# A scan kernel on one core: order of a PSUM seed, two gate tiles kept in SBUF, earlier stores, and group statistics on GpSimd

## The chip, the cores and the metric

The kernel runs on one core of one Trainium2 chip. The metric is device time in microseconds (us) of one execution, the median of several. One more execution was recorded by the profiler; every duration of a single instruction comes from that one.

## What is computed

The input x is 4 x 128 x 96 x 96, float32. It is normalized in 32 groups of channels, then four sequences of each image (rows, rows backwards, columns, columns backwards) go through one block, and the four results are mixed and added to x:

```python
t = _grouped1x1(x, in_proj_w, in_proj_b, G)
u, gate = (t[:, :HID], t[:, HID:])
u = jax.nn.silu(u)
u = lax.conv_general_dilated(u, dw_w, ..., feature_group_count=HID)   # 5 taps
s = _conv1x1(u, ssm_in_w)
a = DMIN + (DMAX - DMIN) * jax.nn.sigmoid(_conv1x1(u, ssm_delta_w, ssm_delta_b))
bb = jnp.tanh(_conv1x1(u, ssm_b_w, ssm_b_b)); cc = jnp.tanh(_conv1x1(u, ssm_c_w, ssm_c_b))
# hst: h[i] = a[i] * h[i-1] + bb[i] * s[i]
u = u + _conv1x1(cc * hst + ssm_d[None, :, None] * s, ssm_out_w)
u = _grouped1x1(u * jax.nn.sigmoid(gate), mix_w, mix_b, G)
return _conv1x1(u, out_proj_w, out_proj_b)
```

## The kernel before

The engines are TensorE (PE), VectorE (DVE), ScalarE (ACT), GpSimd (POOL) and SyncE (SP), whose queue issues nearly all DMAs. The order of every engine's work is written out by hand.

**Pairs, steps, phases.** The work is cut into 192 pairs t = 0 to 191. A pair is the same quarter (residue p of the column index) of a block of lines in two opposite directions, s = 0 and 1. Four pairs (k = 0 to 3, residues 1, 2, 3, 0) make a step, six steps a phase of 24 pairs, and eight phases cover four images, columns (V) before rows (H). Below m = t mod 24. Back-end work (ssm_out, gating, final products) lags by six pairs: in pair t it is that of pair n = t - 6. Front-end work (in_proj and silu) runs four pairs ahead. Pairs 0 to 7 are emitted by `pair`, the others by `pair_on`.

**Fresh and copied steps.** In the first three steps of a phase silu is computed. As the opposite direction sees the same lines in mirrored order, the last three steps reuse it: it is stored to DRAM (`keep_silu`, L473) and loaded again (`load_silu`). The gates, tanh of a projection of x, go the same way: computed in the first half of a phase, stored to `kept`, and in the second half pair n loads that of pair `mirror(n)` (12 takes 9, 13 takes 8, 14 takes 11, 15 takes 10). There are two gate tiles in SBUF, `gates[n % 2]` (`tile_of`, L597). The gates of the first three pairs of the next phase are computed early, in m = 17, 18 and 19, into the tile `shared` and stored from there. A tap that reaches into the neighbouring 32 channels' rows needs copies of silu's edge rows: `keep_lone` (L699) stores them with four DMAs and `load_lone` (L706) loads them into the tile `lone`, which `add_lone` (L710) reads in pairs of k = 2 and 3. `keep_lone` is issued in the pair of k = 0 of a fresh step, and its load in k = 1.

**One pair in `pair_on` (L1044), in PE's order.** If a front is due, in_proj into banks 7, 6, 2, 3; `conv` with the matrix `band`; two `accumulate` calls, the final products of the pair before (`w_fin`), whose results ACT copies to `ys` and POOL adds to `acc`; `conv_less` with the matrix `less`, if the pair is not single (k = 0 and 1), followed by ACT's copy of the sum to u; a block of eight matmuls, four gates and four ssm_out; `proj`, the four projections of u. A pair with a front is called fronted here (m = 20 to 23 and 0 to 7), one that is neither fronted nor single **long** (m = 8, 9, 12, 13, 16, 17), one that is single and not fronted short. ssm_out adds onto a seed: `under` (L557) has ACT copy u into ssm_out's banks (0 and 1 for s = 0, 2 and 3 for s = 1). Banks 0 and 1 are also where DVE sums the taps 1 to 4 (L765), ahead of the seed, after ACT's first tap (L763). `gating` (L649) on DVE multiplies ssm_out with the gate. On ACT a long pair runs: the projections' tanh and copies (L802, L805, L810), the scaling of s (`scale_s`, L820), the seed of s = 1, a ys copy, u's copy (L738), the seed of s = 0 (L560), a ys copy, two tanh of gates (L564), the first tap, two more gates (L570).

**Statistics.** During the V phase of an image, DVE takes bn_stats of the next image's chunks (L412). Then `stats_finish` (L181) is a generator: in each pair of k = 2 and 3 of the following H phase `pair_on` runs two of its pieces between the final products and conv_less, on PE, DVE and POOL (three Newton steps for the inverse root), so that the scaled weights `wn` and biases `bnorm` are there four pairs ahead of the next image.

**SP's order at the end of a pair.** The store of the new gate (L1143, which waits for its last tanh), the x_in loads for later gates (`load_gate`), the chunk of x for the statistics (`load_chunks`), and the gate of pair n + 2 (`load_kept`); after a pair of k = 2 this load goes to the start of the next.

Of the kernel before, what the change touches and what calls it, by code (L numbers as in the profile page):

```python
# [47 lines left out]
P = 128  # L48
# [20 lines left out]
def conv_preact_kernel(  # L69
# [111 lines left out]
    def stats_finish(b):  # L181

        if b != b0:
            yield
# [7 lines left out]
        if b != b0:  # L197
            yield
# [14 lines left out]
        if b != b0:  # L213
            yield
        inv = sp.tile([P, 2], F32, tag="inv", name=f"inv_{b}")
        if b == b0:
            std = sp.tile([P, 2], F32, tag="err", name="std")
            nc.scalar.activation(std, var, AF.Sqrt)

            nc.scalar.activation(first_table, std[:, 0:1], AF.Silu)  # L220
            nc.vector.reciprocal(inv, std)
        else:
            bits = inv.bitcast(I32)
            nc.vector.tensor_single_scalar(bits, var.bitcast(I32), 1, ALU.logical_shift_right)
            nc.vector.tensor_scalar(bits, bits, -1.0, float(0x5F3759DF), ALU.mult, ALU.add)
            err = sp.tile([P, 2], F32, tag="err", name=f"err_{b}")
            for turn in range(3):
                if turn:
                    yield
                    yield  # L230
                nc.gpsimd.tensor_mul(err, inv, inv)
                nc.gpsimd.tensor_mul(err, err, var)
                nc.gpsimd.tensor_scalar(err, err, -0.5, 1.5, ALU.mult, ALU.add)
                nc.gpsimd.tensor_mul(inv, inv, err)
        yield
        if b != b0:
            yield
# [4 lines left out]

# [3 lines left out]


        pb = bank(free[0])
        product(pb[:, 0:4], wn, gm4)
        if b == b0:  # L250
            for g in range(4):
                for q in range(R):
                    mm(pb[:, 4 + g : 5 + g], q, wn[0:32, 32 * g : 32 * g + 32], mean[0:32, :], True, True)
            nc.vector.tensor_sub(bn, b_in, pb[:, 0:8])
        else:
            nc.vector.tensor_sub(bn[:, 0:4], b_in[:, 0:4], pb[:, 0:4])
            spread = sp.tile([P, 4], F32, tag="spread", name=f"spread_{b}")
            shift = sp.tile([P, 1], F32, tag="shift", name=f"shift_{b}")
            nc.vector.tensor_copy(shift, pb[:, 0:1])  # L259
            yield  # L260
            nc.vector.tensor_scalar_mul(spread, gmask, shift)
            yield
            pq = bank(free[0])
            for q in range(R):
                mm(pq[:, 0:4], q, id32, spread, True, True)
            nc.vector.tensor_sub(bn[:, 4:8], b_in[:, 4:8], pq[:, 0:4])
            yield
        nc.vector.tensor_scalar_mul(bn[:, 2:4], bn[:, 2:4], 0.5)


# [307 lines left out]
    def sigmoids(bi, to):  # L578
        bn = stats[units[bi]["b"]][1]
        n = bi // 2  # L580
        gv = gates[n % 2]
# [15 lines left out]
    def tile_of(n):  # L597
        return gates[n % 2]

    def load_kept(n):  # L600
# [3 lines left out]
        if n < NU // 2 - R and m is not None:  # L604
            nc.sync.dma_start(tile_of(n), kept[n // NP % 2][m])
# [120 lines left out]
    def conv_less(i, banks):  # L726
        step, p = units[i]["step"], units[i]["p"]
        sil, k, b0 = blocks(step), less_of(p), min(banks)
        for g in range(4):
            for s in range(2):  # L730
                r = less_rows(s, p)
                mm(bank(b0 + s), g, less[r, p, g, :], columns(step, sil[s][r, g, :], k),
                   False, True)
        if banks == PROJ:
# [164 lines left out]
    later, soon = [], []  # L899
# [14 lines left out]
    def pair(t):  # L914
# [49 lines left out]
        ending = old and t % (2 * NP) > NP + NP // 2  # L964

        def stats_piece(at_end=False):
            if later and k > 1 and at_end == ending and t % (2 * NP) not in (27, 39):
                next(later[0], None)

        if not ahead:  # L970
            free[0] = w[1]
            stats_piece()
# [18 lines left out]
        if ahead:  # L991
            accumulate(waiting.pop(0), w[1], *final)()
            free[0] = w[0]
            stats_piece()
# [13 lines left out]
        if un["order"] == "V" and un["b"] + 1 < B and un["st"] == NS - 1 and k == R - 1:  # L1008
            later[:] = [stats_finish(un["b"] + 1)]
# [20 lines left out]
        if ending:  # L1030
            free[0] = FRONT[0]
            stats_piece(True)
# [11 lines left out]
    def pair_on(t):  # L1044
# [38 lines left out]
        stats_chunks(t)  # L1083
# [30 lines left out]
        if later and k > 1:  # L1114
            free[0] = w[0]
            for _ in range(2):
                next(later[0], None)
        if fronted:
            if not single:
                conv_less(i, banks)  # L1120
            scale_s(i - 2)
# [12 lines left out]
        gate_of(0, 1, 5)  # L1134
        for s in range(2):
            gating(bi, s)
            if s == 0 and gated is not None:
                tanh_one(gated, to, 1, 1, 4)
                tanh_one(gated, to, 0, 1, 5)
        first_tap(i + 2)  # L1140
        if gated is not None:
            tanh_both(gated, to, 0, 6)
            nc.sync.dma_start(kept[gated // NP % 2][gated % NP], to)  # L1143
# [5 lines left out]
        if un["order"] == "V" and un["b"] + 1 < B and un["st"] == NS - 1 and k == R - 1:  # L1149
# [300 lines left out]
```

## Time and profile before

| | us |
|---|---|
| median of 3 runs (1782.19 to 1784.2) | 1783.57 |
| the profiled execution | 1788.7 |
| its span, first to last instruction | 1787.0 |

The granted TensorE clock was 0.997 over the span. 417.89 MB went through the DMA engines. A row of a group or of the timeline names line, engine, operation and `out<-in` tiles. `psum<-u,w_fin` on PE is `accumulate`, `psum<-sil,band` conv, `psum<-sil,less` conv_less, `psum<-x_in,wn` a gate (32*128) or in_proj (32*32), `psum<-t,main` ssm_out, `psum<-u,main` proj. Line 135 is a helper that emits most matmuls, so tiles tell them apart. Each matmul of the program shows as two instructions.

### The profile page before, as it was taken

The numbers are of one execution on the slowest core, as the hardware profiler recorded it, in microseconds if no ns is written. First come the engines' busy times: TensorE is split into PE (matmuls) and PEld (weight loads), VectorE is DVE, ScalarE is ACT, GpSimd is POOL, SyncE is SP. The second block draws the span as 40 slices with busy tenths as digits, with TensorE's granted clock in tenths as the row PEclk, the third lists the DMA queues.
The fourth block names the chain that finished last, engine by engine and source line by source line (L and its number), as shares of the span: only waits on it lengthen the run. The fifth ranks groups of instructions, "written<-read, shape, count | busy, mean of one in ns | idle before, by whom it ended". The sixth has DMA issues, their size and how long they took to land.

```text
span 1787.0 us, 54377 instructions
## 1 busy us (share of the span) xinstructions
PE 1739.9 (97%) x22618; PEld 661.0 (37%) x22618; DVE 1496.9 (84%) x1526; ACT 1492.7 (84%) x2551; POOL 1423.3 (80%) x1477
## 2 busy tenths in 40 slices
PE   6999999999999999999999999999999999999998
PEld 3334333443334433344333443334433343334433
DVE  6888888887889888888778988888877888888887
ACT  4888888888888888888888888888888888888875
POOL 3578788877878878887777888888787888888886
PEclk9999999999999999999999999999999999999999
DMA  7775975558996688456798688744889749756464
GB/s 238 213 248 193 304 232 166 202 189 278 292 335 233 233 261 243 143 198 230 249 329 301 217 276 262 225 160 163 276 257 316 260 151 311 239 183 198 166 208 176
DMA packets 193814, 417.89 MB, mean 234 GB/s; under 512 B 17312, under 2 KB 154912, under 8 KB 193568
## 3 DMA queue, kind: packets, MB, share of 16 engines
q1 hardware_dynamic: 193424, 414.37, 70.5%
q8 instruction: 179, 2.93, 0.7%
q14 instruction: 67, 0.55, 0.1%
q10 hardware_dynamic: 144, 0.04, 0.0%
HBM read 250.58 MB, written 163.76 MB: 232 GB/s over the span
## 4 chain that ended last, share of the span: by engine, by line
PE 81%; DMA 8%; ACT 4%; DVE 3%; POOL 2%; issue 1%; SPq 1%; DVEq 0%; ACTq 0%; POOLq 0%
PE psum L135 68%; PE psum L548 8%; PE psum L528 5%; DMA kept<-shared 2%; DVE psum L765 1%; DMA x_in<-in_xs 1%; DMA out<-acc 1%; DMA lone<-edge 1%; ACT sil L498 1%; DMA edge<-sil 1%; ACT psum L560 1%; DVE u L664 1%; DMA xs<-in_xr 1%; ACT psum L763 1%; ACT shared L564 0%
## 5 line engine op out<-in xcount | busy, mean ns | idle before, releaser
L765 DVE SCALAR_TENSOR_TENSOR psum<-sil,small,psum 128x768 f32<-128x768 f32 x576 | 589.0, 1023 | 51.7 <-ACT psum L763 26.3
L135 PE MATMUL psum<-u,main 128*32 128x384 f32 x6144 | 538.2, 491 | 13.8 <-ACT shared L564 7.2
L135 PE MATMUL psum<-u,w_fin 128*32 128x384 f32 (+1 forms) x6192 | 543.1, 485 | 1.6 <-ACT ys L872 0.4
L664 DVE SCALAR_TENSOR_TENSOR u<-gate,psum 128x768 f32<-128x768 f32 x376 | 341.8, 950 | 181.2 <-PE psum L548 65.8
L891 POOL TENSOR_TENSOR acc<-ys,acc 128x384 f32<-128x384 f32 x375 | 411.2, 1119 | 21.2 <-ACT ys L874 4.5
L845 POOL TENSOR_TENSOR t<-t,t 64x384 f32<-64x384 f32 (+1 forms) x192 | 235.3, 1225 | 137.8 <-DVE t L839 84.3
L135 PEld LDWEIGHTS psum<-u,w_fin 128*32 128x32 f32 x6192 | 194.5, 110 | 313.0 <-issue 233.9
L135 PEld LDWEIGHTS psum<-u,main 128*32 128x32 f32 x6144 | 181.4, 110 | 342.6 <-issue 219.6
L560 ACT COPY psum<-u 128x768 f32<-128x768 f32 x380 | 298.2, 799 | 9.2 <-DVE u L664 4.4
L135 PE MATMUL psum<-sil,band 128*32 128x384 f32 x3072 | 285.5, 488 | 0.3 <-ACT gate L570 0.3
L846 POOL TENSOR_TENSOR t<-t,t 64x384 f32<-64x384 f32 (+1 forms) x192 | 272.3, 1418 | 15.1
L812 POOL TENSOR_SCALAR t<-tm 64x384 f32<-64x384 f32 x191 | 177.1, 927 | 110.3 <-ACT tm L802 84.0
L763 ACT ACTIVATE psum<-sil,small 128x768 f32<-128x768 f32 x191 | 172.5, 903 | 86.0 <-DVE u L664 83.6
L548 PE MATMUL psum<-t,main 32*128 32x384 f32 x1536 | 209.6, 524 | 4.5 <-ACT psum L560 3.3
L813 POOL TENSOR_TENSOR t<-t,tm 64x384 f32<-64x384 f32 x192 | 196.7, 1025 | 16.8 <-ACT t L805 1.6
L765 DVE SCALAR_TENSOR_TENSOR u<-sil,small,psum 128x768 f32<-128x768 f32 x192 | 194.9, 1015 | 6.9
L498 ACT ACTIVATE sil<-psum,bnorm 128x385 f32<-128x385 f32 x384 | 192.2, 584 | 3.9 <-PE psum L135 1.8
L528 PE MATMUL psum<-x_in,wn 32*128 32x384 f32 x768 | 167.9, 495 | 3.6 <-DVE shift L259 1.4
L135 PEld LDWEIGHTS psum<-sil,band 128*32 128x32 f32 x3072 | 89.8, 108 | 171.3 <-issue 60.6
L874 ACT COPY ys<-psum 128x384 f32<-128x384 f32 x281 | 129.5, 477 | 14.9 <-PE psum L135 11.8
L564 ACT ACTIVATE gate<-psum,bnorm 128x384 f32<-128x384 f32 x148 | 85.8, 581 | 57.1 <-PE psum L528 56.8
L802 ACT ACTIVATE tm<-psum,small 128x384 f32<-128x384 f32 x192 | 111.1, 579 | 11.6 <-PE psum L135 3.4
(105 smaller groups left out, 1512.0 us busy)
## 6 DMA issues: line engine op xcount, KB each, us to landing
sil<-sil SPq DMA_DIRECT2D x128, 770.0 KB, 6.5
gate<-kept SPq DMA_DIRECT2D x113, 768.0 KB, 6.2
kept<-gate SPq DMA_DIRECT2D x75, 768.0 KB, 3.6
lone<-edge SPq DMA_DIRECT2D x46, 770.0 KB, 7.3
x_in<-in_xs SPq DMA_DIRECT2D x194, 96.2 KB, 3.9
edge<-sil SPq DMA_DIRECT2D x96, 192.5 KB, 6.9
out<-acc SPq DMA_DIRECT2D x48, 384.0 KB, 7.9
kept<-shared SPq DMA_DIRECT2D x21, 768.0 KB, 5.2
```

The source lines that it names most:

```text
L135: nc.tensor.matmul(o[r, : rhs.shape[-1]], lhsT, rhs, start=start, stop=stop, skip_group_check=True)
L498: nc.scalar.activation(sils[step][:, s, j, g, :], bank(bk)[:, : N + 1], AF.Silu, bias=bn[:, 1:2] if j else bn[:, 4 + g : 5 + g],)
L528: nc.tensor.matmul(bank(to)[:, :N], stats[un["b"]][0][r, s, :], x_in[s][r, q, off : off + N], start=True, stop=True)
L548: nc.tensor.matmul(bank(ssm(bi, s) + j)[:, :N], w_so[r, bass.ts(j, P)], z[r, :], start=bi not in seeded, stop=True, skip_group_check=True)
L560: nc.scalar.copy(psum[:, ssm(bi, s) : ssm(bi, s) + 2, :N], us[bi][:, s])
L664: nc.vector.scalar_tensor_tensor(v, g, 1.0, pz, ALU.add, ALU.mult)
L763: nc.scalar.activation(part, src, AF.Copy, scale=w_tap[:, 0:1])
L765: nc.vector.scalar_tensor_tensor(us[i][:, :, 1, :] if k == K - 1 else part, src, w_tap[:, k : k + 1], part, ALU.mult, ALU.add,)
L813: nc.gpsimd.tensor_mul(ta[0:64, p, :], tb[0:64, :], tm[0:64, :])
L845: engine.tensor_mul(ta[0:64, p, r], tb[64:P, r], ta[64:P, p, r])
L846: engine.tensor_add(tb[0:64, r], ta[0:64, p, r], tb[0:64, r])
L891: adder.tensor_add(part, y, part)
```

## The change

1. In long pairs the seed of s = 0 is issued on ACT ahead of u's copy; `conv_less` can leave the copy out and `copy_u` does it later.
2. `tile_of` shifts by one at the middle of each phase, and the gates of pairs 10 and 11 of a phase (`stays`) are neither stored nor loaded. As written, pairs 11 and 12 then share one tile: the load for pair 12, at the end of pair 10, goes into the tile in which pair 11's gate was written, and pair 11's gating comes behind it in the program. Pair 13's load goes into pair 10's tile, and pairs 14 and 15 read the two tiles as these loads left them. So pairs 11, 14 and 15 of a phase multiply with another pair's gate than before.
3. `keep_lone` moves from the pair of k = 0 to the front of the last quarter, one pair earlier (m = 23, 3, 7), and `load_lone` always comes at k = 0.
4. On SP, chunk loads and x_in loads are issued ahead of the store of the new gate.
5. The statistics of images 1 to 3 run at fixed places in the first eight pairs of the H phase, all products in bank 7, with the small elementwise steps on POOL. `bn_stats` stays in its place in single pairs and comes behind the gatings in the others. The first image's statistics keep their order under the name `stats_first`.
6. The scaling of s at the end of m = 19 moves into the next pair, behind its conv_less.

```diff
-    def stats_finish(b):
...
+    def stats_first(b):
...
+    def stats_finish(b):
...
+        wn, pm = wns[:, 0, :], bank(7)
...
+        def means():
+            product(pm[:, 0:1], gmean, mv[:, 0:1])
+
+        def spreads():
+            nc.vector.tensor_copy(mean, pm[:, 0:1])
+            nc.gpsimd.tensor_sub(dev, mv[:, 0:1], mean)
+            nc.gpsimd.tensor_mul(ex, dev, dev)
+            nc.gpsimd.tensor_add(ex, ex, mv[:, 1:2])
+            nc.gpsimd.tensor_scalar(gm4, gmask, mean, None, ALU.mult)
+
+        def variances():
+            for e in range(2):
+                product(pm[:, e : e + 1], gmeans[:, e, :], ex)
...
+        def scale_w():
+            for e in range(2):
+                nc.gpsimd.tensor_scalar(wns[:, e, :], w_in[:, e, :], inv[:, e : e + 1], None, ALU.mult)
+
+        def biases():
+            product(pm[:, 0:4], wn, gm4)
             for g in range(4):
                 for q in range(R):
+                    mm(pm[:, 4 + g : 5 + g], q, wn[0:32, 32 * g : 32 * g + 32], mean[0:32, :], True, True)
...
+        return {
+            (0, 0): gather,
+            (1, 1): means,
+            (1, 2): spreads,
+            (2, 1): variances,
+            (2, 2): lambda: nc.vector.tensor_scalar_add(var, pm[:, 0:2], GN_EPS),
+            (3, 0): guess,
+            (4, 0): newton,
+            (5, 0): newton,
+            (6, 0): scale_w,
+            (7, 1): biases,
+            (7, 2): finish,
+        }
...
+        if g == R - 1 and fresh(step) and step > 1:
+            keep_lone(step)
...
     def tile_of(n):
-        return gates[n % 2]
+        return gates[(n + (n + NP // 2) // NP) % 2]
+
+    def stays(m):
+        return NP // 2 - 3 < m < NP // 2
...
-        if n < NU // 2 - R and m is not None:
+        if n < NU // 2 - R and m is not None and not stays(m):
             nc.sync.dma_start(tile_of(n), kept[n // NP % 2][m])
...
-    def conv_less(i, banks):
+    def conv_less(i, banks, copy=True):
...
+        if copy:
+            copy_u(i, banks)
...
+    def piece(t, place):
+        later.pop((t % NP, place), lambda: None)()
...
-        if k == 0 and fresh(un["step"]):
-            keep_lone(un["step"])
-        if k == (1 if fresh(un["step"]) else 0):
+        if k == 0:
             load_lone(un["step"])
...
         recurrence(t)
-        stats_chunks(t)
+        piece(t, 0)
+        if single:
+            stats_chunks(t)
...
         if not fronted:
             if not single:
-                conv_less(i, banks)
+                conv_less(i, banks, False)
             under(bi, 0)
+            if not single:
+                copy_u(i, banks)
...
-        if later and k > 1:
-            free[0] = w[0]
-            for _ in range(2):
-                next(later[0], None)
         if fronted:
             if not single:
                 conv_less(i, banks)
+            if t % NP == 20:
+                scale_s(i - 4)
             scale_s(i - 2)
...
         gate_of(0, 1, 5)
+        piece(t, 1)
         for s in range(2):
             gating(bi, s)
...
+        piece(t, 2)
+        if not single:
+            stats_chunks(t)
         first_tap(i + 2)
         if gated is not None:
             tanh_both(gated, to, 0, 6)
-            nc.sync.dma_start(kept[gated // NP % 2][gated % NP], to)
+        if un["order"] == "V" and un["b"] + 1 < B and un["st"] == NS - 1 and k == R - 1:
+            later.update(stats_finish(un["b"] + 1))
+        if t + 2 < end:
+            load_chunks(t + 2)
+        if gated is not None:
             for s in range(2):
                 load_gate(2 * gated + s + UB)
         if t % NP in (14, 15, 16, 17):
             for s in range(2):
                 load_gate(2 * (t + 10) + s)
...
+        if gated is not None and not stays(gated % NP):
+            nc.sync.dma_start(kept[gated // NP % 2][gated % NP], to)
...
-        if not fronted:
+        if not fronted and (t % NP != 19 or t + R >= end):
             scale_s(i - 2)
```

More of the change, by code (lines that the diff above doesn't have):

```diff
@@ L212, in stats_finish @@
         nc.vector.tensor_scalar_add(var, pv[:, 0:2], GN_EPS)
-        if b != b0:
-            yield
         inv = sp.tile([P, 2], F32, tag="inv", name=f"inv_{b}")
[L216 to L234, printed above, removed]
+        std = sp.tile([P, 2], F32, tag="err", name="std")
+        nc.scalar.activation(std, var, AF.Sqrt)
+        nc.scalar.activation(first_table, std[:, 0:1], AF.Silu)
+        nc.vector.reciprocal(inv, std)
         yield
-        if b != b0:
-            yield
         wns = sp.tile([P, 2, P], F32, tag="wn", name=f"wn_{b}")
@@ L251, in stats_finish @@
             for g in range(4):
                 for q in range(R):
[L253 to L267, printed above, removed]
@@ L580, in sigmoids @@
         n = bi // 2
-        gv = gates[n % 2]
+        gv = tile_of(n)
         for s in range(2):
```

58 lines of the change are left out of this document (32 added, 26 removed).

## The prediction

> **What bounds the kernel now.** I read the page first, then the table of waits, then the timeline of TensorE (PE) pair by pair, and last the DMA rows. From the page:
>
> ```profile
> span 1787.0 us, 54377 instructions
> PE 1739.9 (97%) x22618; PEld 661.0 (37%) x22618; DVE 1496.9 (84%) x1526; ACT 1492.7 (84%) x2551; POOL 1423.3 (80%) x1477
> PE 81%; DMA 8%; ACT 4%; DVE 3%; POOL 2%; issue 1%; SPq 1%; DVEq 0%; ACTq 0%; POOLq 0%
> ```
>
> PE is the bound nearly everywhere; the chain that ended last is left to DMA for 8%. No matmul of the main work is added or taken away, so only what PE waits for can be won. The table of waits (total us, times, longest) names the visible part:
>
> ```profile
> PE psum L135 <- ACT shared L564: 7.2, 9, 2.6
> PE psum L135 <- DVE u L717: 4.2, 3, 1.8
> PE psum L548 <- ACT psum L560: 3.3, 7, 0.6
> PE psum L528 <- DVE shift L259: 1.4, 3, 0.5
> PE psum L528 <- DVE bnorm L266: 1.2, 3, 0.4
> ```
>
> The first is the gate computed into `shared`, the second `add_lone`, the third an ssm_out matmul that waits for its seed, the last two the statistics. A wait inside a group of matmuls does not show as idle time. It has to be read from starts. Here is PE in long pair 60 (start us, us), from its conv to that of pair 61, and then ScalarE (ACT) in the same pair:
>
> ```profile
> 565.24 1.47 PE L135 MATMUL psum<-sil,band 128*32 128x384 f32 x16
> ...
> 570.16 0.58 PE L528 MATMUL psum<-x_in,wn 32*128 32x384 f32 x1
> 570.56 0.60 PE L548 MATMUL psum<-t,main 32*128 32x384 f32 x3
> ...
> 572.06 2.79 PE L135 MATMUL psum<-u,main 128*32 128x384 f32 x32
> 574.66 1.47 PE L135 MATMUL psum<-sil,band 128*32 128x384 f32 x16
> ```
>
> ```profile
> 568.91 0.80 ACT L738 COPY u<-psum 128x768 f32<-128x768 f32 x1 [0.37 <-PE psum L135]
> 569.61 0.81 ACT L560 COPY psum<-u 128x768 f32<-128x768 f32 x1
> 570.34 0.48 ACT L874 COPY ys<-psum 128x384 f32<-128x384 f32 x1
> ```
>
> The pair takes 9.42 us. Its block of gate and ssm_out matmuls begins at 570.16, but ssm_out comes only at 570.56: its seed (L560) stands behind u's copy (L738) in ACT's queue and ends at 570.42. The block lasts 1.90 us.
>
> **The change part by part.** *Seed ahead of u's copy.* The seed needs only the last tap on VectorE (DVE), so it can start before conv_less ends. ACT then runs seed, copy, and the ys copy of 570.34 no later than now, because that one waits for PE anyway. What a block costs whose seed is long there, the trace shows where statistics held it back:
>
> ```profile
> 808.02 0.58 PE L528 MATMUL psum<-x_in,wn 32*128 32x384 f32 x1 [0.47 <-DVE shift L259]
> ...
> 809.63 0.53 PE L135 MATMUL psum<-u,main 128*32 128x384 f32 x4
> ```
>
> That is 1.61 us, 0.29 less than 1.90. The wait itself, 570.56 - 570.16 = 0.40, is the upper end. Six of each 24 pairs in eight phases are long, 48, and two more at the end. Between 0.29 and 0.40 I take 0.32: 50 x 0.32 = 16 us. The lower end is 5 us, if a later step of the same chain (DVE's gating, ACT's first tap and tanh, the next conv) leaves 0.1 a pair. [...]
>
> *Statistics.* Pair 75 carries the first piece, pair 51 is the same place without it:
>
> ```profile
> 486.33 1.50 PE L135 MATMUL psum<-sil,band 128*32 128x384 f32 x16
> ...
> 494.92 1.50 PE L135 MATMUL psum<-sil,band 128*32 128x384 f32 x16
> ```
>
> ```profile
> 703.36 1.50 PE L135 MATMUL psum<-sil,band 128*32 128x384 f32 x16
> ...
> 713.01 0.88 PE L135 MATMUL psum<-x_in,wn 32*32 32x385 f32 x16 [0.63 <-DVE u L664]
> 713.82 0.53 PE L135 MATMUL psum<-sil,band 128*32 128x384 f32 x4
> ```
>
> ```profile
> 708.81 1.27 DVE L202 SCALAR_TENSOR_TENSOR ex<-dev,mv 128x1 f32<-128x1 f32 x1
> ```
>
> ```profile
> L231 POOL TENSOR_TENSOR err<-inv 128x2 f32<-128x2 f32 x9 | 1.8, 196 | 0.0
> L135 PE MATMUL psum<-ex,gmean 128*32 128x1 f32 x64 | 1.2, 175 | 0.9 <-ACT ys L874 0.9
> ```
>
> 10.46 against 8.59 us: DVE does tiny steps such as the 1.27 us one ahead of its gating, and the next front waits. With the waits of the other pieces, three batches cost 3 x 1.87 + 0.9 + 1.4 + 1.2 = 9.1 us. In the new order the product follows the out_of matmuls, DVE reads it after its gating, and the small steps go to GpSimd (POOL) at 0.196 us each, a pair or more before the next use. Matmul instructions per batch go from 40 to 64; at an estimated 0.02 us each (175 ns, about eight at once) that is 3 x 0.5 = 1.5. Bank 7 is the new risk: the next front writes it and must wait for DVE's read; gating ends ahead of that front's turn. I take 9.1 - 1.1 (half of the added matmuls and bank waits) = 8 us; the ends are 4 and 9. [...]
>
> *Copied silus stored sooner.* Pair 98 is the worst of the three pairs in which `add_lone` came late:
>
> ```profile
> 912.54 1.50 PE L135 MATMUL psum<-sil,band 128*32 128x384 f32 x16
> ...
> 919.32 4.48 PE L135 MATMUL psum<-u,main 128*32 128x384 f32 x32 [1.78 <-DVE u L717]
> ...
> 924.60 0.85 PE L135 MATMUL psum<-sil,band 128*32 128x384 f32 x8
> ```
>
> ```profile
> lone<-edge SPq DMA_DIRECT2D x46, 770.0 KB, 7.3
> edge<-sil SPq DMA_DIRECT2D x96, 192.5 KB, 6.9
> ```
>
> 12.06 us against 8.59: 1.78 idle, and the projection behind it takes 4.48 where pair 60's took 2.79. The other two pairs have 4.2 - 1.78 = 2.4 us of idle time; 3.47 + 2.4 = 5.9. Store and load in a row take 6.9 + 7.3 us; both now begin one pair (about 9 us) earlier, more than twice any lateness. I take all 5.9; at worst 2. [...]
>
> *Two gates stay in SBUF; SyncE's (SP's) queue.* Pairs 18 and 19 of a phase write `shared` again and wait for its last store:
>
> ```profile
> ACT shared L564 <- DMA kept<-shared: 10.8, 8, 3.1
> ```
>
> ```profile
> 635.41 4.12 PE L135 MATMUL psum<-u,main 128*32 128x384 f32 x32 [1.91 <-ACT shared L564]
> ```
>
> ```profile
> 627.77:640.62 12.85, 10.94 (x132) 4.09 (x125) 10.10 (x11) 8.36 (x15) 9.15 (x10) 0.87 0.93 323
> ```
>
> ```profile
> 627.50 0.34 SPq L1143 DMA_DIRECT2D kept<-shared  x1
> ```
>
> ```profile
> gate<-kept SPq DMA_DIRECT2D x113, 768.0 KB, 6.2
> kept<-shared SPq DMA_DIRECT2D x21, 768.0 KB, 5.2
> ```
>
> The middle row is pair 67: granted clock 0.87, DMA engines full at 323 GB/s. 768 KB at that rate are 2.4 us. Two stores just ahead of these pairs fall away, 4.8 us of queue before the store of 627.50, and two loads behind it. The new order puts x_in and xs loads, some 0.4 MB or 1.2 us, ahead of that store. 3.6 net is more than the longest wait, 3.1. Visible idle is 7.2; pair 67's slow projection (4.12 - 2.79 = 1.3 on 1.9 idle) scales it to 12. I take 10; the ends are 0 and 12.
>
> The same edit adds a wait. The load for pair 12 now goes into pair 11's tile, so it must follow ACT's last tanh of pair 10, and DVE's gating of pair 11 must follow its landing:
>
> ```profile
> 608.89 0.89 ACT L570 ACTIVATE gate<-psum,bnorm 128x768 f32<-128x768 f32 x1
> ```
>
> ```profile
> 616.39 1.82 DVE L664 SCALAR_TENSOR_TENSOR u<-gate,psum 128x768 f32<-128x768 f32 x2 [0.77 <-PE psum L548]
> ```
>
> 609.78 to 616.39 leaves 6.6 us, 6.2 with the faster pair, against a median landing of 6.2. Behind that gating wait ACT's first tap and PE's next pair. I count 0.2 x 8 = 1.6 us lost; the ends are 0 and the rival below.
>
> *The rest.* bn_stats now runs behind the gatings of long and early pairs:
>
> ```profile
> L412 DVE BATCH_NORM_STATS2 bn<-xs 128x6 f32<-128x384 f32 x72 | 39.5, 556 | 3.9 <-DMA xs<-in_xr 3.0
> ```
>
> It pushes the taps of the next pair by up to 0.35 us; where that pair is short (pairs 10, 14, 18 in three phases) its seed is late: 9 x 0.22 = 2 us lost, between 0 and 3. Four edge stores now stand ahead of a gate load in pairs 23, 3 and 7; its landing has some 5 us to spare, cost 0, and 1 us each where that cover is gone. The moved scaling of s is counted at 0: it only changes places on ACT.
>
> Sum: 16 + 8 + 5.9 + 10 - 1.6 - 2 = 36.3 us. The profiled execution took 1788.7 (span 1787.0 and 1.7 around it), 5.1 more than the median 1783.57. 1788.7 - 36.3 = 1752.4; less 5.1 gives **1747.3**, predicted 1747.
>
> **The rivals.** *DMA waits stay.* SP issues in order; edge stores move ahead of gate loads and `shared` stores behind x_in loads, so the waits may only move. For it: DMA share 0.93 in pair 67. Against: 16 stores and 16 loads fewer. The queue terms then give half, 8 of 15.9: 1755.
>
> *The seed was not the bound.* The ys copy of 570.34 ends at 570.82 and frees the bank of the block's last matmul. If that sets its end, 0.1 a pair is left, 5 of 16: 1758. For it: PE shows no idle time there. Against: the 1.61 us block.
>
> *Slower: pair 11 waits for pair 12's gate.* Landings above 6.2 us count in full, and as after pair 98's idle 1.78 (3.47 lost) PE loses twice the lateness. At 8 places a run, 3 us late costs 8 x 6 = 48: 1747 + 48 = 1795. It ends above the time before from about 2.3 us late, a landing of 8.5. For it: the full DMA queue of those pairs. Against: the freed stores.
>
> *No effect.* If the waits only change names, 1783.
>
> **How the numbers follow.** Forecast 0.62, DMA waits stay 0.15, seed not the bound 0.14, pair 11 waits 0.05, no effect 0.04. The forecast's own span is 1737 to 1757, from the ends of the seed and `shared` terms. With the next two rivals the range is 1737 to 1763. A change of 0.2% (3.6 us) is about what can be told from none. Faster 0.62 + 0.15 + 0.14 = 0.91, same 0.04, slower 0.05.
>
> **What would show it.** Right: pair 60's twin takes 9.0 to 9.1 us, with ssm_out starting within 0.1 us of the block; pair 75's takes 8.6 to 8.9; no DVE wait on `lone` and under 2 us of waits on `shared`; DMA bytes down by 32 x 768 KB. Wrong: long pairs above 9.3, new DVE waits on gate loads in pairs 17, or new PE waits on bank 7 after the statistics.

## The result and the profile after

| | us |
|---|---|
| before, median of 4 runs (1782.19 to 1784.62) | 1783.88 |
| after, median of 4 runs (1771.71 to 1774.92) | 1773.55 |
| ratio, with its 95% interval (it isn't formed from the medians) | 0.9928 (0.9903 to 0.9953) |
| the profiled execution of after, and its span | 1771.71, 1769.9 |

The change makes the kernel 10 us faster. The direction was right; the gain is between a quarter and a third of the 36.3 us of the sum, and the time lies outside the range of 1737 to 1763. On two other chips, where the kernel before takes 1789 us, the same kernel came out at 0.9964 (0.9953 to 0.9976) and 0.9946 (0.9925 to 0.9967), 7 to 10 us faster. So below, kernels are compared on one chip, or by their ratio to the kernel before on the same chip. One profiled execution, that of `lone_old` below, took 5951 us at a granted clock of 0.28 and is left out, and `lone_old_2` is the same kernel run once more for its profile.

From the page after:

```profile
span 1769.9 us, 54501 instructions
PE 1727.1 (98%) x22690; PEld 645.3 (36%) x22690; DVE 1480.2 (84%) x1502; ACT 1493.9 (84%) x2550; POOL 1443.0 (82%) x1495
PE 85%; DMA 4%; DVE 4%; ACT 3%; POOL 2%; issue 2%; SPq 1%; POOLq 0%; DVEq 0%; ACTq 0%
```

PE is still the bound, and the chain's DMA share fell from 8 to 4%. First the step that held, long pair 61, PE and then ACT:

```profile
573.65 0.58 PE L551 MATMUL psum<-x_in,wn 32*128 32x384 f32 x1
573.66 0.60 PE L571 MATMUL psum<-t,main 32*128 32x384 f32 x3
...
577.84 1.14 PE L135 MATMUL psum<-sil,band 128*32 128x384 f32 x11
```

```profile
572.34 0.80 ACT L583 COPY psum<-u 128x768 f32<-128x768 f32 x1 [0.31 <-DVE u L796]
573.08 0.79 ACT L769 COPY u<-psum 128x768 f32<-128x768 f32 x1
```

The seed (L583) now ends at 573.14, ahead of the block, and ssm_out starts 0.01 us behind the first gate. Pair 61 takes 9.14 us (568.70, in a row below, to 577.84); the mean of undisturbed long pairs went from 9.43 to 9.11, the 0.32 of the prediction. Pair 75 takes 8.59 in place of 10.46, and 25 MB less were moved (392.72), as the prediction wanted. The table of waits shows where the rest went (total us, times, longest):

```profile
DVE u L690 <- DMA gate<-kept: 16.8, 10, 3.4
...
ACT shared L587 <- DMA kept<-shared: 13.0, 8, 3.3
DVE t L870 <- POOL t L844: 12.9, 9, 2.1
...
PE psum L135 <- ACT shared L587: 8.6, 7, 2.6
PE psum L135 <- ACT gate L593: 8.1, 6, 1.8
...
POOL acc L922 <- DMA acc<-in_xr: 4.1, 2, 2.4
```

The first and the last are new: before, no gating waited for a gate load and no add on POOL waited for a load of acc. The third, DVE's scan waiting for POOL, was 0.3 us in the group of the scan before. The wait on `shared`, which was to fall below 2 us, is 13.0 instead of 10.8. Each is followed below to its cause.

**The load of acc (m = 7 to 12 of the column phases).** SP in pair 55, where the edge stores now stand ahead of gate and acc:

```profile
514.09 2.32 SPq L885 DMA_DIRECT2D out<-acc  x4
516.51 4.16 SPq L728 DMA_DIRECT2D edge<-sil  x4
520.77 0.81 SPq L629 DMA_DIRECT2D gate<-kept  x1
521.62 3.02 SPq L1091 DMA_DIRECT2D acc<-in_xr  x4
```

Then POOL in pair 56, DVE's scan in pair 60, and PE's conv of pair 61:

```profile
531.56 4.73 POOL L922 TENSOR_TENSOR acc<-ys,acc 128x384 f32<-128x384 f32 x4 [2.35 <-DMA acc<-in_xr]
```

```profile
563.05 2.85 DVE L870 TENSOR_TENSOR_SCAN t<-t,t 64x768 f32<-64x768 f32 x1 [2.06 <-POOL t L844]
```

```profile
568.70 1.50 PE L135 MATMUL psum<-sil,band 128*32 128x384 f32 x16 [1.57 <-ACT gate L593]
```

The edge stores take 4.16 us of SP's queue, and the acc load is that much later. POOL starts its four adds 2.35 us late, and it finds no idle time in the next four pairs to catch up (no gap over 0.1 us up to 563.01). The scan of pair 60 needs POOL's product of the projections of pair 59 and waits 2.06; gating, ACT's gates and PE's next conv follow.

**The gate load (m = 4).** In pair 51 the same four stores delay the gate of pair 52, and the gating there waits:

```profile
482.04 3.04 SPq L728 DMA_DIRECT2D edge<-sil  x4
485.17 0.96 SPq L498 DMA_DIRECT2D sil<-sil  x1
486.24 0.58 SPq L631 DMA_DIRECT2D gate<-kept  x1
```

```profile
494.23 1.82 DVE L690 SCALAR_TENSOR_TENSOR u<-gate,psum 128x768 f32<-128x768 f32 x2 [3.18 <-DMA gate<-kept]
```

The gates of m = 0, behind the edge stores of m = 23, are late too: of the 16.8 us in the table 12.9 are in pairs m = 4 and 2.3 in pairs m = 0 of all phases, and in another execution of this kernel (`after_last`) 15.8 and 13.2 of 33.8.

In the stretch around pair 51 the DMA engines are full, before as after. The last two columns of the windows view, here of before and then of after, are their share and the rate:

```profile
450.00:500.00 50.00, 48.64 (x696) 16.91 (x692) 41.06 (x41) 43.19 (x78) 40.42 (x40) 1.00 1.00 322
```

```profile
450.00:500.00 50.00, 49.90 (x724) 17.06 (x724) 42.03 (x42) 43.23 (x79) 39.13 (x37) 1.00 1.02 339
```

**The store of `shared` (m = 17 to 18).** SP at the end of pair 65, ACT's last tanh there and its first of pair 66, and PE:

```profile
612.68 0.35 SPq L429 DMA_DIRECT2D xs<-in_xr  x1
613.12 3.32 SPq L320 DMA_DIRECT2D x_in<-in_xs  x4
616.54 0.53 SPq L1176 DMA_DIRECT2D kept<-shared  x1
```

```profile
612.20 0.88 ACT L593 ACTIVATE shared<-psum,bnorm 128x768 f32<-128x768 f32 x1
...
621.27 1.05 ACT L587 ACTIVATE shared<-psum,bnorm 128x384 f32<-128x384 f32 x2 [3.28 <-DMA kept<-shared]
```

```profile
621.90 4.29 PE L135 MATMUL psum<-u,main 128*32 128x384 f32 x32 [2.61 <-ACT shared L587]
```

The tanh ends at 613.08, the store goes out at 616.54. SP stood at the chunk load until 612.68, because its tile is free only when bn_stats, now behind the gatings, has read it; the four x_in loads behind it take 3.32 us more. In all, SP now stands 83.3 us at chunk loads that wait for bn_stats, where it stood 3.1 us before. The longest wait has moved from m = 19 to m = 18.

**POOL in the row phases (m = 8).** The scan of pair 32 waits for POOL too, and PE for what follows:

```profile
312.94 2.84 DVE L870 TENSOR_TENSOR_SCAN t<-t,t 64x768 f32<-64x768 f32 x1 [1.82 <-POOL t L844]
```

```profile
318.58 0.85 PE L135 MATMUL psum<-sil,band 128*32 128x384 f32 x8 [1.83 <-ACT gate L593]
```

### The profile page after: what moved, and what is told of

The parts are those of the page before. It is cut to its first block, busy times and chain, and to the rows that moved or that the text cites. A ratio compares the mean times of both kernels' runs of the same rounds, so it can differ in the third digit from the quotient of the medians.

```text
span 1769.9 us, 54501 instructions
## 1 busy us (share of the span) xinstructions
PE 1727.1 (98%) x22690; PEld 645.3 (36%) x22690; DVE 1480.2 (84%) x1502; ACT 1493.9 (84%) x2550; POOL 1443.0 (82%) x1495
## 2 busy tenths in 40 slices
DMA packets 189206, 392.72 MB, mean 222 GB/s; under 512 B 16800, under 2 KB 154400, under 8 KB 188960
## 4 chain that ended last, share of the span: by engine, by line
PE 85%; DMA 4%; DVE 4%; ACT 3%; POOL 2%; issue 2%; SPq 1%; POOLq 0%; DVEq 0%; ACTq 0%
PE psum L135 72%; PE psum L571 8%; PE psum L551 5%; DMA kept<-shared 2%; DVE psum L796 1%; DVE u L690 1%; DMA gate<-kept 1%; DMA xs<-in_xr 1%; POOL acc L922 1%; ACT psum L583 0%; DVE u L796 0%; POOL t L844 0%; ACT psum L794 0%; DMA acc<-in_xr 0%; DVE t L870 0%
## 5 line engine op out<-in xcount | busy, mean ns | idle before, releaser
L876 POOL TENSOR_TENSOR t<-t,t 64x384 f32<-64x384 f32 (+1 forms) x192 | 245.6, 1279 | 125.2 <-DVE t L870 105.4
L583 ACT COPY psum<-u 128x768 f32<-128x768 f32 x380 | 298.0, 798 | 15.4 <-DVE u L796 7.7
L877 POOL TENSOR_TENSOR t<-t,t 64x384 f32<-64x384 f32 (+1 forms) x192 | 271.7, 1415 | 15.0
L843 POOL TENSOR_SCALAR t<-tm 64x384 f32<-64x384 f32 x191 | 183.4, 960 | 92.6 <-ACT tm L833 70.3
L571 PE MATMUL psum<-t,main 32*128 32x384 f32 x1536 | 225.4, 524 | 3.6 <-ACT psum L583 2.9
L551 PE MATMUL psum<-x_in,wn 32*128 32x384 f32 x768 | 161.2, 496 | 1.0 <-ACT gate L587 1.0
L853 ACT ACTIVATE t<-t,small 64x384 f32<-64x384 f32 x191 | 117.0, 616 | 8.4 <-POOL t L844 6.0
```

What stands on the lines that cost most here:

```text
L551: nc.tensor.matmul(bank(to)[:, :N], stats[un["b"]][0][r, s, :], x_in[s][r, q, off : off + N], start=True, stop=True)
L571: nc.tensor.matmul(bank(ssm(bi, s) + j)[:, :N], w_so[r, bass.ts(j, P)], z[r, :], start=bi not in seeded, stop=True, skip_group_check=True)
L583: nc.scalar.copy(psum[:, ssm(bi, s) : ssm(bi, s) + 2, :N], us[bi][:, s])
L843: nc.gpsimd.tensor_scalar(*decay(i))
L876: engine.tensor_mul(ta[0:64, p, r], tb[64:P, r], ta[64:P, p, r])
L877: engine.tensor_add(tb[0:64, r], ta[0:64, p, r], tb[0:64, r])
```

## The experiments

The theory from this profile: the seed is worth what was forecast; the edge stores give time back in m = 4 and m = 12 of the column phases, the place of the `shared` store in m = 18, and the new statistics, by way of POOL, in m = 8 of the row phases. Rivals: POOL is saturated whatever the loads do, or the full DMA engines only move the waits. The table has mean lengths of pairs in us, from one conv's start to the next, over the three column phases 2, 4, 6 (V) or the three row phases 1, 3, 5 (H) of each profiled execution; under it the medians and the ratios to before. The kernels are told below; "changed" is the changed kernel on one chip with the three to its right, and a median is compared only there. Each column is one execution. Three executions of the changed kernel (after, after_again, after_last) differ by up to 1.1 us in a row: m = 18 takes 10.61, 10.02 and 11.02, m = 19 takes 9.64, 10.67 and 9.72. In all three, V m = 12 is at 10.06 or more and H m = 8 at 10.47 or more.

| pairs | before | seed_only | changed (after_last) | lone_old_2 | edges7 | old_stats_2 | store_first | best2_again | best3 |
|---|---|---|---|---|---|---|---|---|---|
| V m = 2 | 10.55 | 11.01 | 8.53 | 11.44 | 8.52 | 8.53 | 8.52 | 10.14 | 10.99 |
| V m = 4 | 9.26 | 9.26 | 10.45 | 9.26 | 10.41 | 10.62 | 9.87 | 9.26 | 9.26 |
| V m = 12 | 9.42 | 9.20 | 10.68 | 9.17 | 9.17 | 10.80 | 10.77 | 9.32 | 9.31 |
| V m = 18 | 8.38 | 9.05 | 11.02 | 10.21 | 10.90 | 10.14 | 8.56 | 9.02 | 8.26 |
| V m = 19 | 11.13 | 9.95 | 9.72 | 10.02 | 9.65 | 9.81 | 9.68 | 10.95 | 9.95 |
| H m = 3 | 10.49 | 10.46 | 8.59 | 8.58 | 8.59 | 9.08 | 8.58 | 8.59 | 8.59 |
| H m = 7 | 7.54 | 7.54 | 8.07 | 8.07 | 8.07 | 7.64 | 8.06 | 8.24 | 8.24 |
| H m = 8 | 9.43 | 9.39 | 10.47 | 10.24 | 10.58 | 9.49 | 10.64 | 9.11 | 9.11 |
| H m = 13 | 9.43 | 9.11 | 9.11 | 9.11 | 9.11 | 9.11 | 9.11 | 9.11 | 9.11 |
| median | 1783.57 | 1775.66 | 1779.80 | 1772.03 | 1778.05 | 1779.68 | 1771.04 | 1768.79 | 1762.92 |
| ratio to before | 1 | 0.9905 | 0.9946 | 0.9907 | 0.9936 | 0.9948 | 0.9886 | 0.9887 | 0.9846 |

### The seed alone, and all but the seed

`seed_only` is before with this, `no_seed` the changed kernel with it taken back:

```diff
-                conv_less(i, banks)
+                conv_less(i, banks, False)
             under(bi, 0)
+            if not single:
+                copy_u(i, banks)
```

> The kernel before with the seed of s = 0 ahead of u's copy in long pairs, and nothing else of the change. Theory (the seed term is right in size, and the other edits give part of the gain back): every long pair goes from 9.42 to 9.11 us, 50 x 0.32 = 16 us, so about 1768, below the changed kernel's 1773.6. In column phases the pairs m = 12 stay at 9.1 and POOL does not wait for a load of acc in m = 8. Rival (shorter long pairs let POOL fall behind in column phases): m = 12 of three phases takes 10.3 to 10.9, and 4.6 of the 16 us are lost: about 1772.5.

> The changed kernel with u's copy ahead of the seed of s = 0 again, all other edits as changed. Forecast (the other edits are worth 20 us): 0.989 of the time before. Theory (the seed is worth 16 to 17 us, and the other edits together lose 5 to 10): 1.002 to 1.006 of the time before, so slower than it; long pairs 9.42.

Measured: seed_only 0.9905 (0.9881 to 0.9929) of before, no_seed 1.0022 (1.0006 to 1.0039). The seed alone gains 17 us of the 1792.6 that before takes on that chip, more than the whole change gains anywhere; the other edits together make the kernel slower, by 1 to 7 us. In seed_only the pairs m = 12 of the column phases stay at 9.1 to 9.3, so shorter long pairs alone don't make POOL late: that rival is out. seed_only came at 1775.7 where 1768 was expected, because before was slower on that chip too; the ratio is what the theory said.

### Edge stores and `lone`

`lone_old` and `lone_old_2` are the same kernel, the changed one with the stores at k = 0 and the load at k = 1 of fresh steps again:

```diff
-        if g == R - 1 and fresh(step) and step > 1:
-            keep_lone(step)
...
+        if k == 0 and fresh(un["step"]):
+            keep_lone(un["step"])
-        if k == 0:
+        if k == (1 if fresh(un["step"]) else 0):
             load_lone(un["step"])
```

> The changed kernel with the edge stores and the load of lone back in their places of before (k = 0 and 1 of fresh steps). Forecast (this edit is worth 5.9 us): 0.998 to 1.000 of the time before, with m = 2 of the column phases at 10 to 12. Theory (it wins 6 us in m = 2 and loses 7 in m = 4 and 12): m = 2 as the forecast says, m = 4 at 9.3 and m = 12 at 9.1 to 9.3 in the column phases; 0.992 to 0.996.

> The changed kernel with the edge stores and the load of lone in their places of before, once more, for a profile that can be read. Forecast (early edges are worth 5.9 us): 5.9 us slower than the changed kernel of the same call. Theory (they win 6 us in m = 2 of the column phases and lose 7 or more in m = 4 and 12): 1 to 7 us faster than it; m = 2 at 10 to 12, m = 4 at 9.3 and m = 12 at 9.1 to 9.4.

lone_old: 0.9895 (0.9871 to 0.9920). lone_old_2: 0.9907 (0.9887 to 0.9926), 7.8 us faster than the changed kernel on the same chip. Both come out a little faster than the theory had them. The waits of lone_old_2:

```profile
DVE u L741 <- DMA lone<-edge: 9.0, 3, 3.3
...
DVE u L688 <- DMA gate<-kept: 2.4, 1, 2.4
```

The wait on `lone` is back, as the forecast had it, but the waits on gate loads (33.8 us in the changed kernel on that chip) and those on acc are gone, and these weigh more. In the forecast this edit won 5.9 us.

`edges_behind` issues all early edge stores behind the gate, out and acc transfers of their pair, `edges7` only those of m = 7:

```diff
             reload.clear()
+        if t % NP == 7:
+            keep_lone(step)
         new_u(i)
```

> The changed kernel with the four edge stores of pairs m = 23, 3 and 7 issued behind the gate load, the out stores and the acc loads of the same pair instead of ahead of them. Theory (these stores hold the gate load of m = 4 and the acc load of m = 8 back, and the late acc load makes POOL late for the scan of m = 12): m = 4 of the column phases back to 9.26 (2.4 us in all), m = 12 back to 9.1 (4.6 us), m = 0 back to 9.26: about 1766. Rival (POOL is saturated whatever the load does): m = 12 stays at 10.3 to 10.9, about 1771.

> The changed kernel with only the four edge stores of m = 7 moved behind the gate load, the out stores and the acc loads of that pair; those of m = 23 and 3 stay where the change put them. Theory (edge stores ahead of the acc load make it late, POOL starts pair 8 late and the scan of m = 12 waits for POOL): m = 12 of the column phases at 9.1 to 9.4 and no wait of POOL on the acc load, while m = 4 stays at 9.6 to 11; 4 to 5 us faster than the changed kernel of the same call. Rival (POOL falls behind by the shorter long pairs or the later bn_stats): m = 12 stays above 10.

edges_behind: 0.9903 (0.9876 to 0.9930); m = 12 at 9.1 to 9.4. m = 4 is at 9.26 in two of the three phases, but m = 3 now takes 9.9 to 11.4, where PE waits for x_in (4.4 us in all of this execution, 0.6 in before): the wait had moved, as that rival says. The time is what the theory said as a ratio (1766 of 1783.6 is 0.990), though not pair by pair. edges7: 0.9936 (0.9917 to 0.9956), 1.8 us faster than the changed kernel on its chip, within the intervals, where 4 to 5 were expected. For the mechanism it is clear. SP in pair 55, POOL in pair 56 and the scan in pair 60 of edges7:

```profile
523.21 0.90 SPq L629 DMA_DIRECT2D gate<-kept  x1
524.20 4.37 SPq L1093 DMA_DIRECT2D acc<-in_xr  x4
528.62 3.00 SPq L728 DMA_DIRECT2D edge<-sil  x4
```

```profile
536.07 4.76 POOL L922 TENSOR_TENSOR acc<-ys,acc 128x384 f32<-128x384 f32 x4
```

```profile
567.81 2.81 DVE L870 TENSOR_TENSOR_SCAN t<-t,t 64x768 f32<-64x768 f32 x1
```

Neither POOL's adds nor this scan wait, and m = 12 falls from 10.68 to 9.17 in all three phases, 4.5 us in all; m = 4 stays at 10.4. Of the 4.5 us only 1.8 show in the medians. The two profiled executions are 6.2 us apart (spans 1784.2 and 1778.0), that of the changed kernel being the slowest of its six; why the medians differ by less is open.

### The statistics

`old_stats` and `old_stats_2` are the changed kernel with the generator of before, called with two pieces in pairs of k = 2 and 3:

```diff
-        piece(t, 0)
...
+        if later and k > 1:
+            free[0] = w[0]
+            for _ in range(2):
+                next(later[0], None)
```

> The changed kernel with the statistics of images 1 to 3 in their old form and places (DVE does the small steps, two pieces in each pair of k = 2 and 3). Forecast (the new statistics are worth 8 us): about 1781.5. Theory (they win 10 us in m = 3, 6, 14, 15 and lose 6 to 7 us in m = 7 and 8 of the row phases, where POOL is late for the scan): about 1777, with m = 8 of the row phases at 9.1 instead of 10.3 to 11.3 and m = 3 at 10.5.

> The changed kernel with the old statistics, once more beside the changed kernel on one chip. Forecast: 8 us slower than it. Theory, from the pairs of the first profiles (10 us won in m = 3, 6, 14 and 15 of the row phases, 1.6 lost in m = 7 and 4 to 5 in m = 8): 2 to 4 us slower than it.

old_stats: 0.9948 (0.9930 to 0.9966). old_stats_2: 0.9948 (0.9932 to 0.9964), 0.1 us faster than the changed kernel on its chip. So the new statistics are worth nothing, against 8 us in the forecast and 2 to 4 in the theory. Two things took the gain. One is m = 8, at 9.49 with the old and 10.47 with the new statistics, and m = 7. The other is that the old ones no longer cost what they did: m = 3 takes 9.08 in old_stats_2, not 10.49. The two dear steps on DVE with POOL beside them, first before (the step ahead of them is the 1.27 us of the prediction), then old_stats_2:

```profile
710.00 1.24 DVE L204 TENSOR_SCALAR gm<-gmask,mean 128x4 f32<-128x4 f32 x1
```

```profile
708.84 2.37 POOL L891 TENSOR_TENSOR acc<-ys,acc 128x384 f32<-128x384 f32 x2
```

```profile
712.16 0.52 DVE L202 SCALAR_TENSOR_TENSOR ex<-dev,mv 128x1 f32<-128x1 f32 x1
712.60 0.22 DVE L204 TENSOR_SCALAR gm<-gmask,mean 128x4 f32<-128x4 f32 x1
```

```profile
712.17 0.50 POOL L858 COPY t<-t 64x384 f32<-64x384 f32 x1
712.75 2.39 POOL L901 TENSOR_TENSOR acc<-ys,acc 128x384 f32<-128x384 f32 x2
```

Before, each step begins with one of POOL's two adds and ends with it (1.2 us each); in old_stats_2 POOL is half a microsecond later, still at its copy, and both steps begin ahead of the adds, 1.8 us less for the same two instructions. In all three images the two steps take these times. What makes them long beside the adds, no run shows. Which edit moved POOL was not taken apart; in seed_only the step takes 1.26, so it isn't the seed.

`stats_v2` lets `newton` make all three steps in m = 5, ahead of the recurrence, where POOL waits for the scan (3.20 us in pair 29 of before), and puts the scaling on ACT in m = 6, behind the first tap:

```diff
-                nc.gpsimd.tensor_scalar(wns[:, e, :], w_in[:, e, :], inv[:, e : e + 1], None, ALU.mult)
+                nc.scalar.activation(wns[:, e, :], w_in[:, e, :], AF.Copy, scale=inv[:, e : e + 1])
...
-            (4, 0): newton,
-            (5, 0): newton,
-            (6, 0): scale_w,
+            (5, -1): newton,
+            (6, 3): scale_w,
...
+        piece(t, -1)
         recurrence(t)
```

> The changed kernel with the three Newton steps on POOL all in m = 5, ahead of the recurrence where POOL waits 3.5 us for the scan, and the scaling of the weights on ACT in m = 6 instead of POOL. Theory (in row phases POOL has no idle time from m = 3 to 8 with the new statistics and the scan of m = 8 waits for it): m = 8 of row phases 1, 3 and 5 falls from 10.3 to 11.3 to about 9.2, 4 to 5 us less than the changed kernel of the same call. Rival (the scan of m = 8 is late for another reason): m = 8 stays, within 1 us.

stats_v2: 0.9951 (0.9934 to 0.9969), 2.4 us faster than the changed kernel on its chip (`after_again`, 0.9964, 1782.54), within the intervals; 4 to 5 were expected. Its m = 8 takes 9.44 instead of 10.7, m = 7 8.40 instead of 8.07: 2.8 us net of three phases. The scan's waits for POOL, first in after_again and then in stats_v2, shrink by 5.3 us; of the 6.9 left, 4.8 are in the column phases:

```profile
DVE t L870 <- POOL t L844: 12.2, 10, 1.7
```

```profile
DVE t L869 <- POOL t L843: 6.9, 8, 1.8
```

> The changed kernel, nothing altered, beside the next three on one chip. If the seed alone is worth 16 to 17 us (0.9905 of the time before) and the other edits cancel, it comes out at 0.990 to 0.993 of the time before, the same as the seed alone. If the other edits are worth the 20 us that the prediction gave them, below 0.985.

> The changed kernel, nothing altered, beside the next three on one chip: 0.993 to 0.996 of the time before, as in the two comparisons so far.

after_again came out at 0.9964, above both of its forecasts: the other edits do not cancel but cost something. after_last, at 0.9946, is in its range.

### The store of `shared`, bn_stats and the two gates

`store_first` is the changed kernel with the store ahead of the chunk and x_in loads, `bn_old` with bn_stats ahead of the final products in all pairs, `stays_off` with the tiles and the 16 stores and 16 loads of before:

```diff
             tanh_both(gated, to, 0, 6)
+        if gated is not None and not stays(gated % NP):
+            nc.sync.dma_start(kept[gated // NP % 2][gated % NP], to)
...
-        if gated is not None and not stays(gated % NP):
-            nc.sync.dma_start(kept[gated // NP % 2][gated % NP], to)
```

```diff
         piece(t, 0)
-        if single:
-            stats_chunks(t)
+        stats_chunks(t)
```

```diff
-        return gates[(n + (n + NP // 2) // NP) % 2]
+        return gates[n % 2]
```

> The changed kernel with the store of the new gate issued first at the end of a pair again, ahead of chunk load and x_in loads. Theory (in m = 17 this store stood 3.5 us behind a chunk load that waits for bn_stats and behind four x_in loads, and m = 18 waits for it): the store goes out within 0.5 us of the last tanh, m = 18 falls from 12.9, 10.1 and 10.0 to 8.4, and not more than 3 us come back in m = 19: about 1767. Rival (the DMA engines are full there, and the wait only moves to m = 19 as in the kernel before): about 1773.

> The changed kernel with bn_stats in its old place, ahead of the final products, in all pairs; SP's order as changed. Theory (the chunk load at the head of SP's queue waits for the late bn_stats to free its tile, and the store of the new gate stands behind it): the store of m = 17 goes out within 1.5 us of the last tanh and m = 18 of the column phases falls from 10 to 13 to 9 or less; time like that of the kernel with the store first. Rival (the four x_in loads and full DMA engines hold the store): m = 18 stays above 9.5.

> The changed kernel with the tile order of before and the gates of pairs 10 and 11 stored and loaded again (25 MB more in the DMA engines); all other edits stay. Forecast (this edit is most of a term of 10 us): 8 to 10 us slower than the changed kernel of the same call. Theory (the waits on shared come from the place of the store in SP's queue, not from the volume): within 3 us of it, with m = 18 of the column phases still at 10 to 13, and no wait of DVE on a gate load in m = 17.

store_first: 0.9886 (0.9861 to 0.9912). SP at the end of its pair 65 (the last tanh there ends at 614.88), and its wait on `shared`:

```profile
614.90 0.34 SPq L1166 DMA_DIRECT2D kept<-shared  x1
615.35 0.38 SPq L429 DMA_DIRECT2D xs<-in_xr  x1
```

```profile
ACT shared L587 <- DMA kept<-shared: 1.8, 2, 1.0
```

The store goes out 0.02 us behind the tanh, m = 18 falls to 8.56, and m = 19 (9.68) does not take it back: the 13.0 us of waits of the profile after become 1.8, the "under 2 us" of the prediction. bn_old: 0.9894 (0.9872 to 0.9917), m = 18 at 8.3 to 9.0. There the store still follows the x_in loads, but these go out from 2.2 us ahead of the tanh's end (0.04 behind it in the profile after), since the chunk's tile is free earlier, and the store comes 0.3 us behind the tanh. Either edit cures it. stays_off: 0.9961 (0.9949 to 0.9974) and 1782.90, against 1782.54 of after_again. In the changed kernel the two staying gates are worth nothing, and without them no gating of m = 17 waits for a gate load.

### Versions put together

`best1` joins edges_behind, store_first, bn_old, stats_v2 and stays_off; `best2` has the old places of `lone` in it instead of edges_behind; `best3` is best2 with the two gates staying.

> Seed ahead of the copy; silu edges stored one pair earlier but behind the gate, out and acc transfers of that pair; the store of the new gate first on SP and bn_stats in its old place; the statistics as in the kernel with all Newton steps in m = 5; the gates of pairs 10 and 11 stored and loaded as before. Theory (each stall of the changed kernel goes with its cause): about 5 (m = 12) + 2.5 (m = 4) + 5 (m = 8 of row phases) + 4 (m = 18) less than the changed kernel of the same call, so some 16 us below it, and about 1760 where the kernel before takes 1784. Rival (the DMA engines set the waits, which only move): within 5 us of the changed kernel.

> The best of the call before with the edge stores and the load of lone in their places of before: of the change only the seed, the statistics (Newton steps all in m = 5) and the moved scaling of s are left. Theory (in the first half of column phases the DMA engines are full, and the order of transfers only chooses which pair waits): 6 us back in m = 2, 3 to 5 us gone in m = 3 and 4; 0.987 to 0.990 of the time before, as the best of the call before. Rival (early edges behind the gate load are worth their 6 us): 0.991 to 0.992.

> The best kernel so far, nothing altered, beside the next on one chip: 0.986 to 0.989 of the time before, with 6 to 10 us of waits on shared.

> The same with the tile order and the two staying gates of the changed kernel, so that pairs 11, 14 and 15 of a phase take another pair's gate, as in the changed kernel. Theory (with the store first, 25 MB less in the DMA engines let the stores of m = 17 and 18 land sooner): waits on shared under 3 us, 4 to 6 us faster than the best kernel so far. Rival (the store's place was all): within 2 us of it, waits on shared 6 us or more.

best1: 0.9883 (0.9865 to 0.9900), 15.2 us below after_again. best2: 0.9871 (0.9846 to 0.9896), and again 0.9887 (0.9858 to 0.9917). So early edges, even behind the other transfers, are no better than late ones: best2 loses in m = 2 of the column phases (10.88, best1 8.52), best1 in m = 3 and 4 (10.81 and 10.96, best2 8.61 and 9.26). best3: 0.9846 (0.9819 to 0.9873), 5.9 us below best2_again; the two intervals overlap a little. Waits on `shared`, best2_again and best3:

```profile
ACT shared L584 <- DMA kept<-shared: 11.3, 9, 2.1
```

```profile
ACT shared L584 <- DMA kept<-shared: 5.4, 5, 1.7
```

The wait was expected under 3 us and is 5.4 (in best2_again 6 to 10 were expected), the time is as expected: with the store first the two gates are worth about 6 us. As in the changed kernel, pairs 11, 14 and 15 of a phase then multiply with another pair's gate, so these 6 us price the missing transfers and are no gain for the same result; of the kernels with the gates of before, best2 has the lowest ratio. best3 is 26 us faster than before on its chip, and its interval ends below that of the changed kernel in every comparison.

## Why the prediction was wrong, step by step

| term | forecast | measured | from |
|---|---|---|---|
| seed ahead of u's copy | 16 | 17 | seed_only; 0.32 a long pair |
| statistics | 8 | 0 | old_stats_2 against after_last |
| silus stored sooner, with the stores' new place (counted 0) | 5.9 | -7.8 | lone_old_2 against after_last |
| two gates stay, SP's new order | 10 | 0 to -4 | stays_off 0.4; V m = 18 and 19 together from 19.51 to 20.25, 20.69 and 20.74 |
| pair 11 waits for pair 12's gate | -1.6 | 0 to -1.4 | V m = 17 at 9.25, 9.11 and 9.56 in the three executions |
| bn_stats behind the gatings | -2 | -0.8 | V m = 10 from 8.26 to 8.44, m = 14 to 8.34, three phases |
| scaling of s of m = 19 moved | 0 | about 1.2 | m = 20 from 9.37 (V) and 9.55 (H) to 9.26, three phases each; not run alone |

The measured terms give 4 to 10 us, the three comparisons 6.7 to 10.3. That they meet is in part luck, because the terms were measured in different kernels and do not add: those without the seed give a loss of 7 to 13 us, and no_seed lost 1 to 7.

- **Seed: right**, in mechanism and size. ssm_out stands at the block's start; the rival "the seed was not the bound" is out.
- **The failed step** is the sentence "Four edge stores now stand ahead of a gate load in pairs 23, 3 and 7; its landing has some 5 us to spare, cost 0, and 1 us each where that cover is gone." In m = 7 of the column phases SP needed 3.8 to 4.2 us to issue them, into DMA engines that are full (a share of 0.98 between 516.5 and 520.7 in pair 55), and what stands behind them in pair 7 is the acc load as well. Its reader is POOL, which has no idle time for four pairs; so the delay reappears five pairs later, at the scan. The term of `lone` itself was right (m = 2 did fall from 10.55 to 8.52), and more than all of it was given back in m = 4 and 12 (2.0 us a phase won, 2.2 to 2.8 lost).
- **`shared`: the sum counted bytes ("some 0.4 MB or 1.2 us") where SP's issue counted.** The x_in loads took 3.32 us to issue, and the chunk load at the head waited for bn_stats, which the prediction had moved to later only in DVE's account. store_first, which differs in that order alone, stands at 0.9886, the changed kernel at 0.9928 to 0.9964. The freed traffic does help once the store goes first: 5.9 us in best3.
- **Statistics: right in m = 3, 6, 14 and 15, wrong in price and in cover.** "at 0.196 us each, a pair or more before the next use" holds for the steps themselves; what stands behind them on POOL, the products that the scan of m = 8 needs, was not followed. And the 1.87 us of pair 75 was not the price of the small steps but of their meeting POOL's adds (1.27 and 1.24 us beside them, 0.52 and 0.22 ahead of them in old_stats_2), and most of it went away without the edit (m = 3 at 9.08 in old_stats_2).
- **Pair 11 and bn_stats' push on the taps** stayed within their ends, and the slow rival did not come. The larger cost of the late bn_stats came by way of the chunk load, as told above.
- Of the rivals, "DMA waits stay" was nearest: it took half of the queue terms away; the runs took all of them and more.

## What to carry over

When a DMA is moved ahead in a queue, list every transfer that it is moved past and follow each to its reader and that reader's slack, as far as the next place where engines meet; here a load late by 4 us showed as a stall five pairs on. SP's queue, which issued in order here (the store of 616.54 behind x_in loads that end at 616.44), was priced by issue time (3.32 us for those loads) and by the first semaphore that stopped it, not by bytes. And a combined change should be run edit by edit: one of its edits made all the gain here, and another that looked useless, the two gates, became worth 6 us of time once the order around it was put right, at the price of other gates in three pairs of each phase.

## What the runs showed of the hardware

- In these two executions the length of an idle time does not say what PE loses behind it. In after, behind 1.83 us (row of 318.58), the granted clock stayed at 1.00, and in before, behind 2.63 us (start 200.79), it was 1.00 and the projection took its 2.79 us. In after, behind 2.61 us (row of 621.90), the clock was 0.64 and the projection took 4.29, and in pair 98 of before, behind 1.78, it was 0.62 and the projection took 4.48. What decides between the two, no run shows.
- A DVE step on one column (`ex`, 128x1) took 0.52 us beside a POOL copy of 0.50 (old_stats_2) and 1.27 us beside a POOL add of about 1.2 (before).
